# Layer 2's mixing: when the halves of z are loaded, and where the first poles and masks are made

## The chip, the cores and the metric

The kernel runs on one core of a Trainium2 chip. The metric is the device time of one execution in microseconds (us), the median of several runs. The core has five engines that work side by side, each through its own queue in order: TensorE (PE in the profile; PEld is its weight load), VectorE (DVE), ScalarE (ACT), GpSimd (POOL) and SyncE (SP). SyncE only issues transfers between the chip's memory (DRAM) and the on-chip memory (SBUF); 16 DMA engines carry them out. Matmul results go to PSUM, which VectorE and ScalarE read.

## The reference

The input x has the shape (16, 16, 256, 256): batch, channel, rows, columns. Four layers follow one another, each of the form x = x + layer(groupnorm(x)): a circular 3x3 convolution, a 5-tap diagonal convolution, a Laplace-operator layer (layer 2), and a quantised 3x3 convolution. The change lies in layer 2, of which this is the part concerned:

```python
alpha = jnp.fft.fft2(x, axes=(-2, -1))
A = 1.0 / (omega1[:, None, None, None] - weights_pole1[None])
Bm = 1.0 / (omega2[:, None, None, None] - weights_pole2[None])
S = jnp.einsum('ikpq,oikp,xikq->oxik', weights_residue, A, Bm)
output_residue1 = jnp.einsum('biox,oxik->bkox', alpha, S)
x1 = jnp.fft.ifft2(output_residue1, s=(Ny, Nx), axes=(-2, -1)).real
```

At each of the frequencies (o, x), a 16x16 complex matrix S mixes the channels of alpha, the Fourier transform. The matrices S themselves come from the poles and residues.

## The kernel before, in words

The kernel goes through the layers in stages. The two that matter here are the transform (about 1368 to 2247 us), which computes alpha and leaves it in DRAM as `alphad`, and the mixing (about 2247 to 3141 us), which forms S, multiplies, and leaves the product in DRAM as `mixd`. A later stage transforms back.

In the transform only TensorE's order is written by hand; a scheduler orders the other engines. A generator called `aside` (`sums_over_q`) makes t2, the half of S that depends on x, in small pieces between the transform's own pieces: one piece at every second of the 128 turns, from turn 9.

In the mixing, the order of TensorE, VectorE, ScalarE and GpSimd is the order in which the code is written (a manual schedule), so an instruction that waits holds up whatever is written after it for the same engine.

- **A four.** The stage has 64 steps n (NF = N // 4), each for four rows of frequencies. z holds the alpha of one four: 128 partitions by 8256 numbers, in two buffers z0 and z1 that alternate. Half 0 is the partitions 0 to 63, half 1 the partitions 64 to 127. A half is filled by four loads of 129 KB (line L908), each for 16 partitions. Only blocks of z are loaded; the rest stays zero.
- **A step.** A step goes through 32 places `at`; at each, four products (line L963) multiply a matrix of S, `sk`, with a column of z. They need both halves of z. Eight places fill one PSUM tile ps_m, so a step has four such groups. After each group ScalarE copies half of ps_m to `other` (L978) and VectorE forms sum and difference into ob (two operations on ps_m, line L189, the line of the helper `tt`). ob leaves for DRAM in two stores of 512 KB (L912), at the places 2 and 5 of the next step.
- **Place 8.** A lone product goes to ps_e, VectorE copies it (`alone_`, L987) and GpSimd makes eight small edits with it in ob.
- **The system.** `system(e8)` makes sk for eight rows, that is for two steps: at the places 0, 8, 16 and 24 TensorE multiplies masks `l` with t2 into ps_s (L892), and ScalarE copies the result to sk (L897). The masks are made by GpSimd (`masked`) from the poles af.
- **The poles.** `poles(e8)` makes af, one time in two steps: GpSimd computes e and d (three pieces), VectorE takes the reciprocal g (L855), and eight small products on VectorE make af. In the loop it is a generator `coming`, begun at place 0 of even steps and moved on by one piece at the places 2, 5, 8, 11 and so on. So in even steps its pieces of GpSimd fall on the places 2, 5 and 8, the last of them (ad, py) behind the eight edits of place 8, and the reciprocal on place 11.
- **Loads in the loop.** `moves(n, at)` runs at every place. At the places 0 to 7 of step n it clears one number of z with VectorE (memset, L951) and issues one of the eight loads of z(n+1), half 0 and half 1 by turns. The memset follows the last products that read that buffer, those of step n-1; the load follows the memset. Since the sums of step n-1's last group are written ahead of place 0, they stand ahead of these memsets in VectorE's queue.
- **The head.** Ahead of the loop both buffers of z are cleared (6.97 us each), twelve loads fill z0, the poles of the first two systems and the first masks are made, a constant `alone` is multiplied into two blocks of z0 (L937), and system(0) is made, with the copies to sk shared by ScalarE and VectorE.

## Time and profile before

| what | value |
|---|---|
| median of 3 runs | 4628.29 us (4617.6 to 4630.9) |
| the profiled execution | 4633.67 us |
| its span in the profile | 4631.9 us |
| TensorE busy in the span | 4204.8 us (91%) |
| VectorE, ScalarE, GpSimd busy | 65%, 58%, 47% |
| transform, 1370 to 2247 us | TensorE busy 839.1 of 877 us, VectorE 693.8 |
| head of the mixing, 2247 to 2300 us | TensorE busy 25.1 of 53 us |
| the 64 steps, first product at 2300.06 us | TensorE busy 771.5 of 841 us |
| loads of z | 516 of 129 KB, median 5.3 us to landing |

In the profile, a group of instructions has its line, its engine, its operation and what it writes and reads, out<-in. In the timeline a row begins with start and length; square brackets give how long the engine was idle ahead of it and what ended that. In a table of waits, a row reads "who waited <- for whom: us in total, times, longest". In the table by windows, the columns are the window, its length, the busy time of PE, PEld, DVE, ACT and POOL, the granted clock of TensorE, the busy share of the DMA engines and GB/s. "issue" is a wait that the profile doesn't explain. Times count from the start of the span.

### The profile page before, as it was taken

To read this page: it belongs to the slowest core of one execution; us is meant where nothing else is said; L and a number is where in the kernel's file an instruction comes from. 1 tells how busy PE (TensorE), PEld (TensorE's weight loads), DVE (VectorE), ACT (ScalarE), POOL (GpSimd) and SP (SyncE) were. 2 spreads that over 40 slices of the span, in tenths; PEclk is the share of its full clock that TensorE was granted. 3 is DMA by queue.
4 is the path that set the end of the run, shared out by engine and by line. 5 is a ranking of instruction groups with operands and counts; after the bars stand their busy time and mean duration, and the time that the engine had idled before them with its cause. 6 is when DMAs were issued, how large, how long until landed. Compare 5 with 4: busy or idle time off the path is not lost. (4 is left out here: it accounts for less than half of the span.)

```text
span 4631.9 us, 117927 instructions
## 1 busy us (share of the span) xinstructions
PE 4204.8 (91%) x48400; PEld 3124.5 (67%) x48400; DVE 3029.7 (65%) x5698; ACT 2696.4 (58%) x3689; POOL 2156.4 (47%) x3426
## 2 busy tenths in 40 slices
PE   5999999999849998999799999996899999969999
PEld 1555555555539998999677777775788888834444
DVE  4766676666678787877655555553666666676664
ACT  3786868676424443444387888875444444446664
POOL 1232333323335554545565666554777777731000
PEclk9999999999979999999899999998999999979999
DMA  6676767676335444445266666667878888756664
GB/s 148 151 190 148 192 148 190 151 184 153 95 97 176 140 152 140 154 152 168 61 167 159 156 167 167 159 167 182 219 219 219 219 227 235 220 221 262 272 273 182
DMA packets 414939, 820.26 MB, mean 177 GB/s; under 512 B 41600, under 2 KB 306816, under 8 KB 382592
## 3 DMA queue, kind: packets, MB, share of 16 engines
q1 hardware_dynamic: 357056, 577.54, 46.3%
q0 software_dynamic: 57344, 235.18, 16.1%
q8 instruction: 382, 6.26, 0.6%
q14 instruction: 157, 1.29, 0.1%
HBM read 408.86 MB, written 336.07 MB: 161 GB/s over the span
## 5 line engine op out<-in xcount | busy, mean ns | idle before, releaser
L412 PE MATMUL ps<-va,wt 128*64 128x512 f32 (+1 forms) x1632 | 669.7, 572 | 11.4 <-POOL va L384 9.2
L412 PE MATMUL ps<-vb,wt 128*64 128x512 f32 (+1 forms) x1632 | 667.9, 571 | 4.6 <-DMA vb<-va 4.6
L897 ACT COPY sk<-ps_s 64x516 f32<-64x516 f32 x1008 | 587.6, 583 | 140.0 <-PE ps_s L892 128.3
L892 PE MATMUL ps_s<-t,l 128*128 128x258 f32 x2048 | 529.5, 401 | 27.6 <-POOL l L189 16.4
L756 ACT ACTIVATE y<-ps_y,bc 128x384 f32<-128x384 f32 x512 | 296.8, 581 | 426.5 <-PE ps_y L754 426.5
L250 PE MATMUL ps_c<-q,wt 128*128 128x512 bf16 (+1 forms) x2400 | 503.8, 372 | 17.4 <-DVE q L1203 17.4
L433 ACT ACTIVATE v<-xt,nm 32x2048 f32<-32x2048 f32 x248 | 497.2, 2005 | 9.7 <-PE ps L447 3.5
L447 PE MATMUL ps<-v,w1s 128*64 128x259 f32 x4096 | 485.0, 397 | 11.0 <-DVE v L431 6.7
L892 PEld LDWEIGHTS ps_s<-t,l 128*128 128x128 f32 x2048 | 375.0, 193 | 103.9 <-POOL l L189 20.1
L412 PEld LDWEIGHTS ps<-va,wt 128*64 128x64 f32 x1632 | 223.4, 138 | 311.2 <-issue 284.4
L447 PEld LDWEIGHTS ps<-v,w1s 128*64 128x64 f32 x4096 | 339.0, 142 | 134.5 <-issue 26.2
L250 PEld LDWEIGHTS <-wt 128*128 128x128 bf16 x2400 | 232.9, 97 | 288.1 <-issue 20.4
L189 DVE TENSOR_TENSOR ob<-ps_m,other 128x256 f32<-128x256 f32 x512 | 269.2, 603 | 228.8 <-ACT other L978 222.3
L1092 PE MATMUL ps_o<-exp,fs 128*128 128x128 f32 x2048 | 402.2, 279 | 14.9 <-ACT fs L1138 14.9
L1091 PE MATMUL ps_o<-c_last,zt 128*128 128x128 f32 x2048 | 401.7, 278 | 0.3
L1091 PEld LDWEIGHTS ps_o<-c_last,zt 128*128 128x128 f32 x2048 | 326.8, 195 | 62.9 <-issue 62.3
L963 PEld LDWEIGHTS ps_m<-z,sk 128*32 128x32 f32 x16384 | 253.2, 110 | 156.1 <-issue 108.4
L963 PE MATMUL ps_m<-z,sk 128*32 128x64 f32 x16384 | 297.5, 222 | 66.2 <-issue 30.8
L189 POOL TENSOR_TENSOR w<-rq 128x512 f32<-128x512 f32 x256 | 321.0, 1281 | 28.9 <-ACT rq L1093 26.2
L189 POOL TENSOR_TENSOR acc<-acc,prod 128x256 f32<-128x256 f32 x240 | 228.1, 950 | 218.5 <-DVE prod L189 211.7
L1092 PEld LDWEIGHTS ps_o<-exp,fs 128*128 128x128 f32 x2048 | 316.6, 195 | 16.0 <-ACT fs L1138 15.8
L751 PE MATMUL ps_y<-c_y,qd 128*128 128x128 f32 x2048 | 316.9, 278 | 0.0
(335 smaller groups left out, 8724.6 us busy)
## 6 DMA issues: line engine op xcount, KB each, us to landing
xt<-x2d SPq DMA_DIRECT2D x256, 512.0 KB, 4.3
z<-alphad SPq DMA_DIRECT2D x516, 129.0 KB, 5.3
xt<-in_x_dram SPq DMA_DIRECT2D x256, 256.0 KB, 7.0
x2d<-x2s POOLq DMA_DIRECT2D x256, 256.0 KB, 5.0
mixd<-ob SPq DMA_DIRECT2D x128, 512.0 KB, 5.2
ot<-mixd SPq DMA_DIRECT2D x256, 256.0 KB, 7.3
x3d<-xt POOLq DMA_DIRECT2D x128, 512.0 KB, 5.7
xt<-x3d SPq DMA_DIRECT2D x64, 1024.0 KB, 8.9
```

Of the source, the lines that this page charges most:

```text
L189: eng.tensor_tensor(o, a, b, op)
L250: nc.tensor.matmul(o, lhsT=w, rhs=src, start=i == 0, stop=i == len(work) - 1)
L412: nc.tensor.matmul(ps[halves[h], lo:hi, :], lhsT=wt0[:, w, :], rhs=v[:, 2 * t + lo : 2 * t + hi, j : j + N], start=j == 0 and k == 0, stop ...
L433: nc.scalar.activation(to, o.xt[c][q_], AF.Identity, bias=o.g.nm[q_, 1:2])
L447: nc.tensor.matmul(ps[halves[h], k, 0:U], lhsT=o.w1[:, w : w + 64], rhs=v1[:, lo : lo + U], start=first_, stop=not first_)
L751: nc.tensor.matmul(to[:, :, a, :], lhsT=v[:, c, a, i % 2, :], start=a == 0, stop=a == 1, rhs=y1[:, a].rearrange("p (r f) -> p r f", r=2))
L756: nc.scalar.activation(y[:, c, :], ps[:, 0 : 3 * P], AF.Copy, scale=bc2[:, b, i // 2, 0:1])
L892: nc.tensor.matmul(ps[:, d, 0 : 2 * NX], lhsT=ls[h][:, k + d - k0], rhs=t2[:, h, k + d].rearrange("p x r -> p (x r)"), start=True, stop=True)
L897: copy(sks[2 * e8 + n][64 * h : 64 * h + 64, :, 2 * k : 2 * k + 4] .rearrange("p x (k r) -> p x k r", r=2), ps[64 * n : 64 * n + 64, :, 0 ...
L963: nc.tensor.matmul(to, lhsT=sk[:, x_], rhs=z[:, :, x_], start=True, stop=True)
L1091: nc.tensor.matmul(ps[:, a, c, :], lhsT=zts[d][:, a, c, :], rhs=last[:, c, :], start=True, stop=False)
L1092: nc.tensor.matmul(ps[:, a, c, :], lhsT=fs[:, d, a, :], rhs=ey[:, d, c, :], start=False, stop=True)
```

## The change

The places at which the loads of z are released move. The loads of half 0 of z(n+2) are released in step n, after the last products of place 31 and ahead of the last group's sums; those of half 1 of z(n+1) at place 12 of step n. Before the loop, z(1) is loaded whole. The poles of the first two systems and the first masks are made in the transform, by `prepared`, which continues `aside`; from turn 81 on `aside` moves at every turn. af and l live in a pool `head`, with one buffer for each of two names in place of two buffers for one name; made in the transform, the poles use the room of the masks l01 and l11 for e and d, and need no PSUM. In the head, the two clearings of z0 are cut by columns in place of partitions, z1 is cleared ahead of system(0), and the multiply by `alone` stands after the sixth of system(0)'s eight pieces. z0's second clearing moves from the start of step 1 to the end of step 0. `poles` and `masked` do the same operations as before.

```diff
+    head = between.enter_context(tc.tile_pool(name="head", bufs=1))
+
+    def poles(e8, pool=None, psum=None):
+        af = afs[e8] = new(head, [HC, 2, C, FC], f"af{e8 % 2}")
+        if pool:
+            e, d = new(pool, [HC, C, FC], "ae"), new(pool, [HC, C, FC], "ad")
+        else:
+            e, d = (new(head, [KC, FC, 2, 8], f"l{h}1").rearrange("p k f r i -> p (k f r i)")[:, 0 : HC * C * FC]
+                    .rearrange("p (h k f) -> p h k f", h=HC, k=C) for h in range(HC))
+        g = psum.tile([P, HC, C, FC], F32, tag="ps_g", name="ps_g") if psum else d
...
+            l = new(head, [KC, FC, 2, 8], f"l{h}{k0 // KC % 2}")
...
+        def prepared():
+            yield from sums_over_q(qp, ps_a)
+            for e8 in range(2):
+                yield from poles(e8)
+            masked(0, 0)
+            yield
+
         before, accs, due = None, [], []
-        aside = sums_over_q(qp, ps_a)
+        aside = prepared()
...
-            if n > 7 and n % 2:
+            if n > 7 and (n % 2 or n > 80):
                 next(aside, None)
...
+        def halfload(n, h):
+            if n < NF:
+                z = zs[n % 2]
+                for f in range(4):
+                    V.memset(z[64 * h : 64 * h + 64, 4 * f, 0, 0:1], 0.0)
+                    load(n, h, f, f)
...
-        V.memset(zs[0][0:64], 0.0)
-        first, second = poles(0), poles(1)
-        for _ in range(3):
-            next(first)
-        Q.memset(zs[0][64:P], 0.0)
+        V.memset(zs[0][:, 0 : FB // 2], 0.0)
+        Q.memset(zs[0][:, FB // 2 :], 0.0)
         for h in range(HC):
             for f in range(4):
                 for to in ((0, 1) if f < 2 else (f,)):
                     load(0, h, f, to)
-        for _ in first:
-            pass
-        masked(0, 0)
-        for _ in second:
-            pass
-        for to in range(2):
-            block = zs[0][:, 4 * to : 4 * to + 4]
-            V.tensor_scalar(block, block, alone[:, to : to + 1], None, MUL)
-        for _ in system(0):
-            pass
         Q.memset(zs[1], 0.0)
-        def moves(n, at):
-            if n and at in (2, 5):
-                leave(n - 1, at // 3)
-            if n == 1 and at == 0:
-                Q.memset(zs[0][:, 0:8], 0.0)
-            if n + 1 < NF and at < 8:
-                h, f = at % 2, at // 2
-                V.memset(zs[(n + 1) % 2][64 * h : 64 * h + 64, 4 * f, 0, 0:1], 0.0)
-                load(n + 1, h, f, f)
+        for at, _ in enumerate(system(0)):
+            if at == 5:
+                for to in range(2):
+                    block = zs[0][:, 4 * to : 4 * to + 4]
+                    V.tensor_scalar(block, block, alone[:, to : to + 1], None, MUL)
+        halfload(1, 0)
+        halfload(1, 1)
...
-                    coming = poles(n // 2 + 2)
-                moves(n, at)
+                    coming = poles(n // 2 + 2, ep, ps_p)
+                if n and at in (2, 5):
+                    leave(n - 1, at // 3)
+                if n and at == 12:
+                    halfload(n + 1, 1)
                 if at % GX == 0:
                     next(steps, None)
                 for a in range(4):
                     product(ps[32 * a : 32 * a + 32, at % GX], 1 + PX * a + at)
+                if at == PX - 1:
+                    if n == 0:
+                        Q.memset(z[:, 0:8], 0.0)
+                    halfload(n + 2, 0)
```

More of the change, by code (lines that the diff above doesn't have):

```diff
@@ L661, in sums_over_q, with masked @@
         yield
+    afs, lss, sks = {}, {}, {}
+    KC = 4
+    NE = N // FC
+    head = between.enter_context(tc.tile_pool(name="head", bufs=1))
[7 more added lines that the diff above has]
+        g = psum.tile([P, HC, C, FC], F32, tag="ps_g", name="ps_g") if psum else d
+        for h in range(HC):
+            tt(Q, e[:, h], bc(wy[:, FC * e8 : FC * e8 + FC], 1, C), bc(pyi[:, h], 2, FC), SUB)
+        yield
+        tt(Q, d, e, e, MUL)
+        yield
+        tt(Q, d, d, bc(py2, 3, FC), ADD)
+        yield
+        V.reciprocal(g, d)
+        yield
+        for k, at in enumerate(blocks):
+            tt(V, af[at, :, 1 - k % 2], e[at], g[at], MUL)
+            yield
+            tt(V, af[at, :, k % 2], g[at], bc(pyr, 3, FC)[at], MUL)
+            yield
+    def masked(e8, k0):
+        if e8 == NE:
+            return
+        ls = []
+        for h in range(HC):
+            l = new(head, [KC, FC, 2, 8], f"l{h}{k0 // KC % 2}")
+            for r in range(2):
+                a = afs[e8][:, h, r, k0 : k0 + KC]
+                tt(Q, l[:, :, :, r], bc(a, 3, 8), bc(bc(mod, 1, FC), 1, KC), MUL)
+            ls.append(l.rearrange("p k f r i -> p k (f r i)"))
+        lss[e8, k0] = ls
     with ExitStack() as es:
@@ L799, in project @@
             V.tensor_copy(gall[:, b, :], ps)
+        def prepared():
[3 more added lines that the diff above has]
+            masked(0, 0)
+            yield
         before, accs, due = None, [], []
-        aside = sums_over_q(qp, ps_a)
+        aside = prepared()
         order = [(b0 + b, i) for b0 in range(0, B, BG) for i in range(0, C, 2) for b in range(BG)]
@@ L832, in layers @@
         zp = es.enter_context(tc.tile_pool(name="c_z", bufs=1))
-        fp = es.enter_context(tc.tile_pool(name="c_f", bufs=2))
-        lp = es.enter_context(tc.tile_pool(name="c_l", bufs=2))
         sp = es.enter_context(tc.tile_pool(name="c_s", bufs=4))
@@ L840, in layers @@
         FB = 4 * B // BG
-        def poles(e8):
-            af = afs[e8] = new(fp, [HC, 2, C, FC], "af")
-            e, d = new(ep, [HC, C, FC], "ae"), new(ep, [HC, C, FC], "ad")
-            g = ps_p.tile([P, HC, C, FC], F32, tag="ps_g", name="ps_g")
-            for h in range(HC):
-                tt(Q, e[:, h], bc(wy[:, FC * e8 : FC * e8 + FC], 1, C), bc(pyi[:, h], 2, FC), SUB)
-            yield
-            tt(Q, d, e, e, MUL)
-            yield
-            tt(Q, d, d, bc(py2, 3, FC), ADD)
-            yield
-            V.reciprocal(g, d)
-            yield
-            for k, at in enumerate(blocks):
-                tt(V, af[at, :, 1 - k % 2], e[at], g[at], MUL)
-                yield
-                tt(V, af[at, :, k % 2], g[at], bc(pyr, 3, FC)[at], MUL)
-                yield
-        KC = 4
-        NE = N // FC
-        afs, lss, sks = {}, {}, {}
-        def masked(e8, k0):
-            if e8 == NE:
-                return
-            ls = []
-            for h in range(HC):
-                l = new(lp, [KC, FC, 2, 8], f"l{h}")
-                for r in range(2):
-                    a = afs[e8][:, h, r, k0 : k0 + KC]
-                    tt(Q, l[:, :, :, r], bc(a, 3, 8), bc(bc(mod, 1, FC), 1, KC), MUL)
-                ls.append(l.rearrange("p k f r i -> p k (f r i)"))
-            lss[e8, k0] = ls
         def system(e8):
```

## The prediction

> **What bounds the kernel now.** I read the page first for the engines' shares and then left it, because its chain of waits covers only the end of the span. The change touches one stage, layer 2's mixing. The records of the products ps_m put it at 2300 to 3141 us. A stage of 64 equal steps is best read by its steps, so I took the start of each step n, s(n), as the start of its first product. The table by windows gives the steps 2 to 59 together, two single neighbours, and the last two:

> ```profile
> 2327.93:3095.17 767.24, 714.24 (x16820) 567.23 (x16821) 415.21 (x1243) 625.93 (x1158) 467.73 (x1041) 0.98 0.65 162
> 2873.42:2885.40 11.98, 11.98 (x291) 9.60 (x291) 5.83 (x20) 10.81 (x21) 7.85 (x18) 1.00 0.69 179
> 2885.40:2897.38 11.98, 11.98 (x291) 9.60 (x290) 6.68 (x20) 10.82 (x21) 8.32 (x18) 1.00 0.69 179
> 3118.93:3141.20 22.27, 10.49 (x516) 9.33 (x516) 8.65 (x26) 2.98 (x8) 4.89 (x16) 0.85 0.49 145
> ```

> The second column is TensorE's busy time. An undisturbed step is 11.98 us with TensorE never idle; 767.24 us over 29 pairs of steps is 26.46 us a pair, so 2.5 us of each pair is disturbance. The waits of TensorE in the stage say which:

> ```profile
> PE ps_m L963 <- issue: 30.8, 24, 3.8
> PE ps_m L963 <- DMA z<-alphad: 30.2, 16, 3.8
> PE ps_m L963 <- DVE z L951: 4.8, 7, 1.2
> ```

> Sixteen stalls wait for the landing of z. So the question is when each half of z is asked for, and that is decided by VectorE, whose tiny memset stands ahead of each load and releases it. Step 14 (s = 2486.81) in the timeline of VectorE, then of GpSimd:

> ```profile
> 2488.41 1.09 DVE L189 TENSOR_TENSOR ob<-ps_m,other 128x256 f32<-128x256 f32 x2 [1.67 <-ACT other L978]
> 2490.23 0.21 DVE L987 COPY alone__21701<-ps_e 32x64 f32<-32x64 f32 x1 [0.73 <-PE ps_e L963]
> ...
> 2493.95 1.76 DVE L855 RECIPROCAL ps_g<-ad 128x256 f32<-128x256 f32 x1 [3.51 <-POOL ad L189]
> ```
> ```profile
> 2490.52 0.24 POOL L189 TENSOR_TENSOR e<-alone__21701 32x32 f32<-32x32 f32 x1 [2.47 <-DVE alone__21701 L987]
> ...
> 2493.30 0.62 POOL L189 TENSOR_TENSOR ad<-ad,py 128x256 f32<-128x256 f32 x1
> ```

> The reader is to see the chain: TensorE's lone product (place 8) lets VectorE copy `alone` at s+3.42; GpSimd then does eight small edits, and only then the addition that the reciprocal needs. VectorE stands still 3.51 us in front of the reciprocal, which runs from s+7.14 to s+8.90. All even steps show this, at +7.1 unless the step is disturbed; odd steps have no reciprocal. Over the stage:

> ```profile
> DVE ps_g L855 <- POOL ad L189: 105.8, 30, 4.1
> ```

> Today this idle time costs little, since the loads were released at the start of the step.

> [...] VectorE idles 3.51 us with later work ready. [...] here the issue takes 0.37 us (median) and the landing comes 2.7 to 8.6 us later. [...] the records here do show half clock in pieces of 3.41 us, but stalls of 1.8 to 2.4 us[...] already brought some.

> **The change, part by part.**

> *Half 1 of z(n+1), even steps.* It moves from the start of step n to place 12. In the order of the compiled program, its four memsets in even steps stand right behind the reciprocal (place 11) on VectorE. They can't start before s+8.90; memset and issue add 0.1 (memset 2300.72, first issue 2300.80 in the trace): s+9.0. Four loads then land one after the other. The nearest case is the first four of z(1), with nothing else queued:

> ```profile
> L908 SPq DMA_DIRECT2D z<-alphad x4: 302/370/917, 2300.8 to 2302.7; - x4
> DMA to landing us min/median/max: 3.1/3.7/4.2
> ```

> The fourth is issued 1.9 us after the first and lands 4.2 later: 6.1 us. By s+9 the queue is empty again (half 0 landed, both stores of ob gone by about s+8), so I take 6.1; below, 5.0 (faster issue, landings 0.75 apart as in busy steps); above, 6.7 (landings 1.05 apart after a slow start, as in the 12 first loads). So z(n+1) is whole at s+15.1, and TensorE starts 0.1 to 0.4 after a landing: 15.3 against 11.98. Each of the even steps 2 to 58 ends in a stall of 3.3 us that nothing hides, because TensorE's queue holds next only the products that need z.

> *The clock after it.* The three stalls above 2.4 us were each followed by half clock. This is the one after 3.76 us:

> ```profile
> 2514.60 1.94 PE L963 MATMUL ps_m<-z,sk 128*32 128x64 f32 x64 [3.76 <-DMA z<-alphad]
> 2516.47 3.81 PE L892 MATMUL ps_s<-t,l 128*128 128x258 f32 x8
> ```

> 1.94 stands for 1.10 and 3.81 for 2.01. The steps behind those stalls took 13.61, 13.61 and 14.72 where 11.98 is the floor. I take 1.65 in 9 of 10: +1.5 a pair (0.5 to 2.5).

> *Odd steps.* No reciprocal, so half 1 goes out after `alone`, at s+3.5 (5.1 at half clock), and lands by s+11.2 at the latest: no stall. Half 0 is released ahead of the four's last sums, about 2 us sooner than today, and lands by s+5. Its memsets wait for TensorE's last product, but the sums queued behind them wait for that product too: nothing lost. In SP's queue the stores of ob now stand between the halves and are served in time.

> *The pair.* 11.98 + 15.3 + 1.5 + 0.2 (the issue waits of odd steps; those of even steps, about 0.7 a pair, fall into the new stall) = 29.0, against 26.46: +2.5, times 29 = **+73 us**. With the ends of the unknowns: 27.2 to 30.1, +21 to +105.

> *The head.* Today the first product comes at 2300.06, because memset, poles, masks, and system matrices follow one another from 2252.7:

> ```profile
> 2252.66 6.97 POOL L925 MEMSET z<- 64x8256 f32 x1 [1.86 <-PE ps_g L798]
> 2254.53 6.94 DVE L921 MEMSET z<- 64x8256 f32 x1 [1.66 <-issue]
> ...
> 2261.39 1.70 DVE L855 RECIPROCAL ps_g<-ad 128x256 f32<-128x256 f32 x1
> ```

> After: both z0 memsets halve (3.54 each, the row of 128x4128), and the first four of 16 groups of copies start near 2256.5, since their masks exist. But GpSimd now clears all of z1 (6.98) before the second masks: 2252.7 + 3.5 + 7.0 + 2.4 = 2265.6. From 2265, twelve groups at 1.31 us (16 took 20.9), the `alone` multiply 2.5 and 1.2 to the first product: 2284.4. That is −15.7; I take −15 (−10 to −18).

> *The transform before it* takes in two poles and one set of masks: VectorE 2 × (1.7 + 8 × 0.42) = 10 us, GpSimd about 6. VectorE is busy 694 of 877 us there and TensorE 839, so it is mostly hidden: +2 (0 to 10, all of it if the cover fails).

> *Ends.* z0's second clearing (3.5 us on GpSimd) now stands between step 0's last product and half 0 of z(2), with VectorE's last sums waiting behind it: step 1 +2. Steps 60 to 63 have no reciprocal and ask for half 0 earlier: −3.

> Sum: +73 − 15 + 2 + 2 − 3 = **+59 us**. The span is 4631.9 and that execution took 4633.67, so it would take 4693; the median shown is 5.4 lower, so I give 4628.3 + 59 = **4687 us**.

> **The rivals.** *Milder:* the four loads land in 5.0 us and the clock drops every second time. Stall 2.2, pair 27.2, +21; with the ends about 4636. For it: the queue is empty at s+9. Against: every lone group of loads in the trace landed about 1 us apart. *Faster, the other side:* all z waits vanish. That needs half 1 released by about s+5.7 (11.98 − 6.1 − 0.2) in even steps too; if the reciprocal didn't hold the memsets, 35 us of waits for z, some 6 half-clock penalties of 1.65 and the head's 15 would go: about 4568. For it: the odd steps reach that. Against: the 3.51 us wait, in all even steps, and the order on VectorE. *Worse:* even steps leave VectorE so late (half 0's memsets near s+14) that in odd steps half 1, queued behind the stores of ob, misses s+11.98 too, by 1.5: +43 more, 4730.

> **How the numbers follow.** The likeliest 0.71, own range 4655 to 4712; milder 0.14, worse 0.08, faster 0.07. 0.3% (14 us) is about what a measurement tells from no change. Milder straddles that bound at 4642, so half of it is "same": slower 0.86, same 0.07, faster 0.07. Leaving out faster and worse, and a little of both tails, the range is 4636 to 4712.

> **What would show it.** In the profile after: even steps of about 15.3 us with one wait of some 3 us for DMA z before the first product of each odd step; first issue of half 1 at s+9.0, just after the reciprocal; total wait for z near 95 us; PEclk with many 3.41 us pieces of half clock; odd steps free of waits for z; first product near 2284. It is wrong if the reciprocal starts well before s+7, if four loads land within 3 us, or if the stalls bring no half clock.

## The result, and the profile after

The changed kernel takes 4697.4 us (median of four runs, 4687.2 to 4706.0) against 4627.2 us (four runs, 4617.6 to 4630.9). The ratio is 1.0154, with a 95% interval of 1.0128 to 1.018. It is slower by 70 us, and it lies within the range that was given. The profiled execution of the changed kernel was its fastest (4687.19 us, span 4685.3), and that of the kernel before lay above its own median (4633.67). So the two traces differ by 53 us of span where the medians differ by 70. The comparison of the traces below accounts for the 53.

In the code after, the products are L964, the masks' products L903, the copies to sk L908, the copy `alone_` L995, the reciprocal L686, the memsets of z L931 and its loads L919. The table by windows of the kernel after, for the same four stretches as before: the steps 2 to 59, an even step (20), the odd step after it, and the last two steps. The second column is TensorE's busy time, the column after the engines is the granted clock.

```profile
2322.39:3153.30 830.91, 732.09 (x16821) 581.47 (x16821) 402.92 (x1247) 625.70 (x1158) 467.82 (x1041) 0.96 0.66 150
2578.19:2593.23 15.04, 12.05 (x292) 9.62 (x291) 8.92 (x25) 12.39 (x23) 7.71 (x17) 1.00 0.55 132
2593.23:2606.83 13.60, 13.60 (x290) 10.82 (x291) 4.87 (x19) 9.23 (x18) 7.84 (x18) 0.87 0.76 167
3176.47:3197.97 21.50, 11.74 (x516) 10.62 (x516) 8.38 (x23) 2.98 (x8) 5.24 (x20) 0.84 0.61 165
```

The 58 steps now take 830.91 us in place of 767.24. The first line also tells idle time and longer work apart. At full clock and without waits 58 steps keep TensorE busy for 58 × 11.98 = 694.8 us. After, it was busy 732.1, which is 37.3 more. The record of the granted clock has 16 pieces of half clock (0.50) in these steps, 64.8 us in all. TensorE worked through nearly all of that time, so they make some 30 of the 37.3; the rest is in steps with waits and no half clock. The other 830.9 − 732.1 = 98.8 us it stood still. Before, the same sums give 19.4 (six pieces, some 11 us) and 53.0. So 45.8 us of the growth is standing still, and the 17.9 of longer work is what the ten more pieces of half clock explain.

The two lines in the middle show the form of it. The even step is 15.04 long with 12.05 of work: 3 us of standing still at full clock. The odd step is 13.60 long and has no gap, but its clock is 0.87. Over the stage even steps went from 13.17 to 15.24 us on average, odd ones from 13.28 to 13.41.

The waits of TensorE in the kernel after, from 2280 to 3170 us (who waited <- for whom: us, times, longest):

```profile
PE ps_m L964 <- DMA z<-alphad: 43.4, 15, 3.4
PE ps_m L964 <- DVE ob L189: 42.6, 15, 3.4
PE ps_m L964 <- issue: 13.5, 18, 1.9
```

The first two rows are 30 stalls, 2.9 us on average: one at the end of each of the even steps 2 to 58, and one in step 1. They are 1.3 to 3.4 us long; most of the short ones have an "issue" wait earlier in the same step. Half of them are put down to VectorE's `ob`. That name misleads. The products wait for several things at once, and in all 29 even steps, whichever name the row gives, they start 0.24 to 0.40 us after z's last load has landed. Step 20 (s = 2578.19) shows the chain, first in VectorE's timeline, then in the loads of z of that step, then in TensorE's timeline:

```profile
2581.61 0.21 DVE L995 COPY alone__23143<-ps_e 32x64 f32<-32x64 f32 x1 [0.20 <-PE ps_e L964]
2585.33 1.76 DVE L686 RECIPROCAL ps_g<-ad 128x256 f32<-128x256 f32 x1 [3.51 <-POOL ad L189]
2587.15 0.08 DVE L931 MEMSET z<- 64x1 f32 x4
```
```profile
L919 SPq DMA_DIRECT2D z<-alphad x4: 317/371/944, 2587.2 to 2589.1; - x4
...
DMA to landing us min/median/max: 3.1/3.7/3.8
```
```profile
2588.23 2.01 PE L903 MATMUL ps_s<-t,l 128*128 128x258 f32 x8
2593.23 1.52 PE L964 MATMUL ps_m<-z,sk 128*32 128x64 f32 x64 [2.99 <-DMA z<-alphad]
2594.68 3.21 PE L903 MATMUL ps_s<-t,l 128*128 128x258 f32 x8
```

The reciprocal starts at s+7.14 behind the same wait of 3.51 us for GpSimd, the memsets follow at s+8.96, the first load at s+9.05, the last lands at s+14.80, and TensorE resumes at s+15.04. The 1.52 and 3.21 behind the stall are 1.10 and 2.01 at full clock.

The head of the mixing after, on GpSimd, VectorE and TensorE (timelines):

```profile
2261.42 3.54 POOL L941 MEMSET z<- 128x4128 f32 x1 [1.23 <-PE ps_g L842]
2264.90 6.98 POOL L946 MEMSET z<- 128x8256 f32 x1
```
```profile
2261.40 0.29 DVE L843 COPY gall<-ps_g 128x128 f32<-128x128 f32 x1 [0.58 <-PE ps_g L842]
2262.50 3.50 DVE L940 MEMSET z<- 128x4128 f32 x1 [0.81 <-issue]
```
```profile
2294.35 1.10 PE L964 MATMUL ps_m<-z,sk 128*32 128x64 f32 x64
```

The last copy of the transform, to `gall`, ends the stage before; it came at 2252.58 before and comes at 2261.40 now. From it to the first product it took 47.5 us and takes 33.0. So the head is 14.5 us shorter, but it begins 8.8 us later. The table by windows of the kernel before and then of the kernel after shows where those 8.8 arise, in the first turns of the transform (after the window and its length come the busy times of PE, PEld and DVE):

```profile
1400.00:1420.00 20.00, 20.00 (x181) 20.00 (x180) 18.49 (x33) 9.27 (x20) 13.42 (x13) 1.00 0.55 178
1420.00:1440.00 20.00, 20.00 (x181) 20.00 (x180) 15.32 (x29) 9.28 (x20) 11.66 (x12) 1.00 0.57 177
```
```profile
1400.00:1420.00 20.00, 17.24 (x146) 16.32 (x145) 18.34 (x32) 7.69 (x15) 11.69 (x15) 1.00 0.60 190
1420.00:1440.00 20.00, 15.95 (x134) 15.00 (x133) 19.85 (x34) 7.35 (x15) 11.70 (x13) 1.00 0.48 158
```

Though the code asks for the new poles in the last turns, the scheduler put their two reciprocals at 1377.0 and 1419.9 us and their products at 1407 to 1436, where VectorE had little room. VectorE is full (19.85 of 20 us in the second window). TensorE waits for VectorE's output `al` ten times between 1370 and 1445 us, 7.7 us in all (before: once, 1.2), and is busy 2.8 and 4.1 us less in these two windows. By 1440 us the kernel is some 10 us behind, and 800 us later 8.8 of it is still there. The point where a transform ends differs by some us between runs of the same code: 2257.0 to 2266.0 us in the six traces with these early poles, 2248.9 to 2252.7 in the four without. But in each of the six, and in none of the four, TensorE falls 11 us behind the kernel before between 1390 and 1432 us.

The sum of the mixing in the traces: steps 2 to 59 +63.7, transform +8.8, head −14.5, steps 0 and 1 +0.2, last four steps −1.3: +56.9, of which the later stages gave back 3.5.

### The profile page after: what moved, and what is told of

It reads as the page before. It is cut to its first block, busy times and chain, and to the rows that moved or that the text cites. A ratio compares the mean times of both kernels' runs of the same rounds, so it can differ in the third digit from the quotient of the medians.

```text
span 4685.3 us, 117912 instructions
## 1 busy us (share of the span) xinstructions
PE 4219.0 (90%) x48400; PEld 3138.5 (67%) x48400; DVE 3017.1 (64%) x5698; ACT 2698.1 (58%) x3689; POOL 2155.8 (46%) x3426
## 5 line engine op out<-in xcount | busy, mean ns | idle before, releaser
L908 ACT COPY sk<-ps_s 64x516 f32<-64x516 f32 x1008 | 587.5, 583 | 137.1 <-PE ps_s L903 118.1
L903 PE MATMUL ps_s<-t,l 128*128 128x258 f32 x2048 | 538.9, 407 | 14.8 <-DVE sk L908 8.0
L189 DVE TENSOR_TENSOR ob<-ps_m,other 128x256 f32<-128x256 f32 x512 | 271.7, 609 | 307.2 <-ACT other L986 298.2
L903 PEld LDWEIGHTS ps_s<-t,l 128*128 128x128 f32 x2048 | 382.6, 197 | 93.7 <-DVE sk L908 10.2
L964 PE MATMUL ps_m<-z,sk 128*32 128x64 f32 x16384 | 307.6, 227 | 110.1 <-DMA z<-alphad 46.5
L964 PEld LDWEIGHTS ps_m<-z,sk 128*32 128x32 f32 x16384 | 262.4, 113 | 200.0 <-DVE ob L189 105.2
L189 POOL TENSOR_TENSOR w<-rq 128x512 f32<-128x512 f32 x256 | 320.6, 1279 | 31.4 <-ACT rq L1101 28.6
L189 POOL TENSOR_TENSOR acc<-acc,prod 128x256 f32<-128x256 f32 x240 | 228.4, 952 | 220.7 <-DVE prod L189 214.2
```

The source lines that it names most:

```text
L189: eng.tensor_tensor(o, a, b, op)
L903: nc.tensor.matmul(ps[:, d, 0 : 2 * NX], lhsT=ls[h][:, k + d - k0], rhs=t2[:, h, k + d].rearrange("p x r -> p (x r)"), start=True, stop=True)
L908: copy(sks[2 * e8 + n][64 * h : 64 * h + 64, :, 2 * k : 2 * k + 4] .rearrange("p x (k r) -> p x k r", r=2), ps[64 * n : 64 * n + 64, :, 0 ...
L964: nc.tensor.matmul(to, lhsT=sk[:, x_], rhs=z[:, :, x_], start=True, stop=True)
```

## Experiments

The theory of the prediction: the reciprocal in front of half 1's memsets, held by GpSimd's last addition, which stands behind the eight edits, sets the end of every even step. The rival (P) says that place 12 itself is too late in the step, so that a transfer issued there never fits. A second one puts the loss on the head. Changes are shown against the kernel after, unless said. Each ratio is to runs of the kernel before taken beside the experiment: their median is 4631.3 us for the first four and 4627.4 for the last four.

**Half 1 two places earlier.**

```diff
-                if n and at == 12:
+                if n and at == 10:
                     halfload(n + 1, 1)
```

> The changed kernel with one number altered: half 1 is released at place 10 in place of 12, so its memsets stand between the lone copy of place 8 and the reciprocal of place 11 on VectorE. Theory R (the reciprocal, which waits for GpSimd, holds the memsets): half 1 goes out at about s+3.6 in even steps, lands by s+9.9, and even steps fall from 15.2 to about 12.0, odd steps to about 12.3 with the half clock gone. A pair of steps takes 24.3 in place of 28.65 us, over 29 pairs -126 us: about 4570 us, below the kernel before. Rival P (place 12 is simply too late in the step, four loads behind one another don't fit in the rest of it): two places are about half a microsecond of TensorE's time, so even steps fall by about 0.5 us and the kernel takes about 4675 to 4685 us.

Measured: 4649.1 us (4645.4 to 4659.3, 7 runs), ratio to the kernel before 1.004 (1.0023 to 1.0056). It takes back 48 of the 70 us, but not the gain that was expected. Even steps fell to 13.66 us, and odd ones stood at 13.47. The stall of the even steps is gone: half 1 goes out at s+3.8 in nearly all of them. A part of it has come back in the odd steps. The windows of steps 2 to 59, VectorE across the start of step 15 (s = 2500.74), and TensorE at its end:

```profile
2325.51:3112.34 786.83, 720.68 (x16820) 571.41 (x16821) 399.70 (x1247) 626.62 (x1158) 469.31 (x1041) 0.98 0.68 158
```
```profile
2501.68 0.41 DVE L189 TENSOR_TENSOR af<-ps_g,pyr 32x256 f32<-32x256 f32 x1
2502.15 0.08 DVE L931 MEMSET z<- 64x1 f32 x4
```
```profile
2515.67 1.33 PE L964 MATMUL ps_m<-z,sk 128*32 128x64 f32 x64 [2.88 <-DMA z<-alphad]
```

Half 0 is released behind place 31 of the even step. In VectorE's queue its memsets stand behind the late reciprocal, the products of the poles and the sums that all slipped with it; they run at s+1.4 of the odd step in place of s−1.9. Its loads go out from s+1.5, the stores of ob behind them from s+3.7, and half 1, third in SyncE's queue, lands at s+14.6. In the kernel after this lateness is hidden, since TensorE's own stall of 3 us gives VectorE time to catch up: there half 0 goes out at s−1.5 in odd steps.

**The reciprocal behind half 1's memsets, place 12 kept.**

```diff
-                if at % 3 == 2:
+                if at and at % 3 == 0:
                     next(coming, None)
```

> The changed kernel with half 1 left at place 12, and the pieces of the poles moved from the places 2, 5, 8, 11, ... to 3, 6, 9, 12, ..., which puts the reciprocal just behind half 1's memsets on VectorE. The reciprocal itself still waits for GpSimd until about s+7.1. Theory R: even steps fall to about 12.0 us, as if the loads had moved, about 4570 us. Rival P (place 12 itself is too late): no change, even steps stay at 15.2 us, about 4697 us.

Measured: 4648.0 us (4635.2 to 4664.9, 18 runs), ratio 1.0039 (1.0027 to 1.0052); even steps 13.61, odd 13.95. Place 12 is kept and the even step's stall of some 3 us is gone all the same, so rival P falls: the place was not too late. But the time is that of the first experiment, not the one expected. Half 1 goes out at s+3.8 to 4.5 in most even steps. The reciprocal behind it makes VectorE late, half 0 goes out at s+0.5 to 1.4 of the odd steps 21 to 25, and half 1 behind it is whole at s+12.7 to 13.9. Both experiments missed in the same way. Taking the hold off half 1 alone is worth some 50 us; the rest needs VectorE to be on time.

**GpSimd's last addition ahead of the eight edits.**

```diff
-                if at % 3 == 2:
+                if at % 3 == 1:
                     next(coming, None)
```

> The changed kernel with half 1 left at place 12 and the pieces of the poles at the places 1, 4, 7, 10, ...: the reciprocal still stands ahead of half 1's memsets, but GpSimd's last addition for it is written ahead of the eight edits of place 8 in place of behind them. Theory R, with the wait and not the reciprocal's own 1.76 us as the larger part: the reciprocal runs from about s+3.6 to s+5.4, half 1 goes out at s+5.5 and lands at s+11.3 to 11.6, just in time. Even steps 12.0 to 12.3 us, the kernel about 4570 to 4590 us. If order behind the reciprocal is what costs, whatever the reciprocal waits for, even steps stay near 15 us. Rival P: no change, about 4697 us.

Measured: 4589.0 us (4588.6 to 4593.9, 4 runs), ratio 0.9909 (0.989 to 0.9927). Even steps 12.44, odd 12.62. VectorE in step 16 (s = 2499.66), and the waits of TensorE that hide a landing of z, from 2280 to 3055 us:

```profile
2503.08 0.21 DVE L995 COPY alone__22174<-ps_e 32x64 f32<-32x64 f32 x1 [0.17 <-PE ps_e L964]
2503.22 1.74 DVE L686 RECIPROCAL ps_g<-ad 128x256 f32<-128x256 f32 x1
2505.01 0.08 DVE L931 MEMSET z<- 64x1 f32 x4
```
```profile
PE ps_m L964 <- DMA z<-alphad: 3.9, 2, 3.6
PE ps_m L964 <- DVE ob L189: 0.8, 2, 0.4
```

The edit moves every piece of the poles one place forward. VectorE's order around half 1's memsets stays, but the addition falls on place 7 in place of 8, in front of the eight edits. The reciprocal has no wait in front of it, and starts at s+3.56 in place of s+7.14. The reciprocal still stands ahead of the memsets on VectorE. It no longer hurts, because it isn't late: from step 4 on half 1 goes out at s+5.4 and is whole by s+11.0 to 12.2, and half 0 goes out at about s−1.8 in both kinds of steps. TensorE waits for z four times, not 30: 3.6 us in step 1, and three times 0.4 us. This one line turns +1.5% into −0.9%. So what cost the time is the wait of VectorE for GpSimd: with it gone, the reciprocal's 1.76 us ahead of the memsets and place 12 itself cost next to nothing.

**The loop's reciprocal twice.** The value is computed a second time into the same tile.

```diff
         V.reciprocal(g, d)
+        if pool:
+            V.reciprocal(g, d)
```

> The changed kernel with the reciprocal of the loop's poles computed twice in a row into the same place (the second gives the same numbers), so the memsets of half 1 come 1.76 us later in even steps and nothing else changes its order. Theory R: each even step grows by 1.76 us to 17.0 us, 29 of them by 51 us, half clock about as often as now or a little more: about 4745 to 4760 us. If the stall has another cause (rival P), VectorE has the room for 1.76 us in a pair of steps and the kernel stays within about 10 us of 4697 us.

Measured: 4753.6 us (4749.1 to 4757.1, 4 runs), ratio 1.0261 (1.0241 to 1.0281). The even step grew from 15.24 to 17.04: by 1.80 for 1.76 us added. In the changed kernel VectorE's queue up to the memsets is on the critical path, us for us. The odd step grew by 0.3 us as well, for now half clock followed all 29 stalls; the granted clock over the steps 2 to 59 was 0.93, where the kernel after had 0.96.

**The loop's releases alone.** The transform and the head are those of the kernel before; `moves` goes, and the halves are released as in the kernel after (against the kernel before):

```diff
-        def moves(n, at):
...
+        halfload(1, 0)
+        halfload(1, 1)
...
-                moves(n, at)
+                if n and at in (2, 5):
+                    leave(n - 1, at // 3)
+                if n and at == 12:
+                    halfload(n + 1, 1)
...
+                if at == PX - 1:
+                    if n == 0:
+                        Q.memset(z[:, 0:8], 0.0)
+                    halfload(n + 2, 0)
```

> The kernel before with the loop's releases of z alone changed (half 0 behind place 31, half 1 at place 12, z(1) loaded whole ahead of the loop); poles, masks, clearings and head as before. If the loop and the head add up, as the traces say (transform 9.4 us later, head 14.5 us shorter): 4697 + 5 = about 4702 us, even steps 15.2 us. If the even steps' stall comes from the head's part of the change (other buffers for af and l), the kernel stays near 4630 us.

Measured: 4698.6 us (4694.3 to 4702.4, 4 runs), ratio 1.0152 (1.0132 to 1.0172); pair of steps 28.75. The whole loss, 71 us, is here.

**The transform's and the head's part alone.** The kernel after with `moves` put back in the loop:

```diff
-        halfload(1, 0)
-        halfload(1, 1)
+        def moves(n, at):
...
-                if n and at in (2, 5):
-                    leave(n - 1, at // 3)
-                if n and at == 12:
-                    halfload(n + 1, 1)
+                moves(n, at)
...
-                if at == PX - 1:
-                    if n == 0:
-                        Q.memset(z[:, 0:8], 0.0)
-                    halfload(n + 2, 0)
```

> The changed kernel with the loop's loads as they were before (by turns at the places 0 to 7, z0's second clearing at the start of step 1): first poles and masks in the transform, and the new head, alone. By the traces: transform +9.4, head -14.5, so 5 us faster than before, about 4623 us. By the prediction's own terms (transform +2, head -15): 13 us faster, about 4615 us. Pairs of steps as before, 26.5 us.

Measured: 4626.7 us (4616.6 to 4640.1, 14 runs), ratio 0.9995 (0.9984 to 1.0007). The head's −14.5 and the transform's +8.8 would leave −5.7, which the interval (−7 to +3 us) holds; a gain can't be told from none. The 13 us that the prediction's own terms give are ruled out.

**The new poles held back in the transform.** One input of the poles gets, times zero, a number of an image that exists only late in the transform, so that the scheduler can't start them before; the turns at which `aside` moves are set accordingly.

```diff
         def prepared():
             yield from sums_over_q(qp, ps_a)
+            hold = new(head, [1], "hold")
+            Q.tensor_scalar(hold, gall[:, 11, 0:1], 0.0, None, MUL)
+            Q.tensor_scalar(pyi.rearrange("p h k -> p (h k)"), pyi.rearrange("p h k -> p (h k)"), hold, None, ADD)
+            yield
...
-            if n > 7 and (n % 2 or n > 80):
+            if n > 7 and (n % 2 and n < 94 or n > 100):
```

> The changed kernel with the two poles and the masks of the transform held back by data: a number of gall that image 11's projection leaves is multiplied by zero and added to pyi, which the poles read (two small GpSimd operations more); the pieces follow from turn 101 on. So the scheduler can't put the poles at the transform's start, where VectorE has no room. If their place is what cost 9.4 us: the transform ends about 7 to 9 us sooner and the kernel takes about 4688 us. If VectorE's extra 10 us cost the same wherever they stand: 4697 us.

Measured: 4679.0 us (4670.3 to 4685.7, 6 runs), ratio 1.0108 (1.0089 to 1.0127); 18 us under the kernel after. The reciprocals run at 2048 and 2065 us. TensorE's window of the early turns is whole again:

```profile
1420.00:1440.00 20.00, 20.00 (x182) 20.00 (x181) 16.02 (x30) 9.43 (x20) 12.17 (x13) 1.00 0.57 185
```

The transform ends at 2252.70 us, as before the change, and the first product comes at 2285.1. In the trace the edit is worth the 8.7 us that the early poles had cost. The medians say 18, but the intervals of the two ratios (1.0089 to 1.0127 here, 1.0128 to 1.018 for the kernel after) leave room for 9.

**Put together.** Addition ahead of the edits, half 1 at place 9, and the poles held back: the diffs of the third and the last experiment, and

```diff
-                if n and at == 12:
+                if n and at == 9:
```

> Three edits to the changed kernel together: the poles' pieces at the places 1, 4, 7, 10, ... (as in the run with the sum early, 4589 us), half 1 at place 9, ahead of the reciprocal, and the transform's poles held back as in the run above. If VectorE's lateness behind the reciprocal is the whole cause, no step has a wait for z left: half 1 at s+3.6 in all steps, half 0 at s-1.9, pairs of about 24.6 us in place of 25.06 (-13 us over 29), and the transform 8 us shorter: about 4568 us. If the last half microsecond of a pair is something else, about 4580 us.

Measured: 4573.8 us (4570.2 to 4575.4, 4 runs), ratio 0.9882 (0.9862 to 0.9901): 54 us faster than the kernel before, 124 faster than the kernel after. Place 9 brings half 1 out at s+3.8 in place of s+5.4 and changes nothing (25.10 us a pair, 25.06 without it), since hardly anything waited for z any more. What it gains over the third experiment lies ahead of the loop: the first product comes at 2282.5 us in place of 2295.4. What TensorE still waits for in the mixing (2280 to 3045 us), and the queue q8 in the steps 2 to 59:

```profile
PE ps_m L968 <- issue: 17.3, 25, 1.7
PE ps_m L968 <- DMA z<-alphad: 3.3, 1, 3.3
```
```profile
q8 instruction: 134, 2.20, 1.6%
```

The one wait for z is that of step 1, behind z0's second clearing. Half clock is all but gone: one piece of 3.41 us in the steps 2 to 59, where the kernel after had 16. So the excess over 23.96 us a pair is mostly "issue". These waits are in every kernel here, and the traces show what comes ahead of them. Queue q8, which the profile labels "instruction", moved 134 transfers of 16 KB in the steps 2 to 59. In these steps of the kernel before and the kernel after TensorE has 20 and 16 "issue" waits longer than 0.25 us, and all 36 end 1.2 to 1.9 us after such a transfer has ended; a random moment lies 1.1 to 1.9 us after one in 13 to 14% of the cases. No run moved these transfers, so the cause of the waits isn't shown.

## Why the prediction was right, point by point

**The pairs of steps: +73 foretold, +63.7 in the trace, +71 between the medians where the loop stands alone.** The mechanism held step by step: reciprocal at s+7.14, memsets behind it, first load at s+9.05 (s+9.0), TensorE back at s+15.0 to 15.5 (15.3). The wait for z came to 86.0 us (43.4 and 42.6) where 95 was foretold. The added reciprocal and the earlier addition show that the hold is the cause, and the second experiment, with place 12 kept, puts rival P out.

Of the terms, the landing took 5.9 us on average (5.7 to 6.2) rather than 6.1. (A load's issue takes 0.38 us at the median, not 0.37; nothing rests on it.) Standing still came to 98.8 us over 29 pairs where 3.5 × 29 = 101.5 was foretold. The clock's term was the one too large. Half clock was foretold behind nine stalls in ten, at 1.65 us each: 1.5 us a pair. It followed 15 of the 29, and those odd steps worked 1.4 to 2.9 us longer: 0.9 a pair. Of the other 14 odd steps six took 11.98 us. Eight took 12.4 to 15.8 us, seven of them with "issue" waits, one of which half clock followed too. All waits within odd steps came to 0.3 us a pair where 0.2 was foretold.

**Odd steps: no stall, rightly, but for an incomplete reason.** The forecast let half 0 go "about 2 us sooner than today" in all steps, as "nothing lost". The first two experiments show that it can be released only as early as VectorE gets there. In the kernel after the even step's own stall pays for that. Half 1 came as late as s+13.1 in odd steps, not by s+11.2, but only in steps that were themselves stretched; from step 3 on at least 1.3 us were left before the next step.

**The head: −15 foretold, −14.5 measured.** The poles and the first masks are off its path, and the second clearing on GpSimd is on it, as worked out.

**The transform: +2 (0 to 10) foretold, +8.8 measured.** In proportion, this term was sized most wrongly. The step at fault is "VectorE is busy 694 of 877 us there and TensorE 839, so it is mostly hidden". An average over 877 us says nothing of where a scheduler puts 10 us of work that is ready at the start. It put the work into a stretch where VectorE had little room: before the change VectorE was busy 18.49 of 20 us from 1400 us on, and 15.32 in the next 20. The head's "first product near 2284" was off by that too: it came at 2294.35.

**Ends: step 1 +2 foretold, and steps 0 and 1 together grew by 0.2; the last four steps −3 foretold, −1.3 measured.** The clearing of z0 does bring a stall of 2.7 us in step 1, but the kernel before already waited 3.6 us for z there, so nothing was added.

**The sum: +59 foretold, +57 by the parts in the traces, +70 between the medians.** The pairs came out 9 us under the forecast and the transform 7 us over it. That the parts sum so well is in part luck.

**The rivals.** Milder and worse didn't come. The faster one named the right condition, half 1 released by about s+5.7, but as put, "if the reciprocal didn't hold the memsets", it fails: without that hold the kernel takes 4649 us, not 4568. With the hold harmless, because the addition comes earlier, it takes 4589, and with the poles held back as well 4574. The mechanism of "worse", half 0 late behind VectorE, is real. It appears when the even stall is gone, and not on top of it.

## What to carry to other kernels

A tiny instruction that releases a transfer inherits every wait ahead of it in its engine's queue (here 3.51 us of waiting and 1.76 us of reciprocal): before moving it, find what stands in front of it there and what that waits for, and price the landing from there. Idle time on an engine that costs nothing today becomes a cost when a release is put behind it (here 45.8 us more of standing still on TensorE in the 58 steps). When one such stall is taken away, look at the other transfers released by the same engine, because the lateness is still there (in the first experiment half 0's memsets ran at s+1.4 of an odd step in place of s−1.9); remove its source (here one place, for one addition on GpSimd) rather than step around it.

## What the runs showed of the hardware

With the reciprocal twice the stalls of the even steps were 3.8 to 5.3 us long, and half clock followed all 29. No run set the place of a stall on the grid on purpose, so these are measured coincidences, and what causes half clock isn't shown.

Four loads of 129 KB on a queue that had run empty, issued within 1.3 to 2.5 us, landed as a row: the first 2.8 to 4.4 us after its issue, the last 5.7 to 6.2 us after the first issue, in all 29 even steps of the kernel after. The prediction's lower end of 5.0 us took landings 0.75 us apart, as in the busy steps of before; it was never reached.
